# Attention stage: column sums through one shared PSUM bank, a split reciprocal, and a new DRAM order of the Q and K halves

## The chip, the cores and the metric

The kernel runs on one core of a Trainium2 chip. The metric is the device time of one execution in microseconds, as a median of runs. The engines named below are TensorE (PE, with its weight loads as PEld), VectorE (DVE), ScalarE (ACT), GpSimd (POOL) and SyncE (SP). SP does no arithmetic here; it issues all the DMAs. The core has 16 DMA engines.

## The reference

Two layers, each behind a group normalisation and with a residual. The first is a Mamba block (a scan over 4,096 positions, then an MLP), which the change does not touch. The second is self-attention over the same 4,096 positions, 8 heads of 32 channels, 2 images:

```python
x = x + _L0_conv_ref(_gn(x), ...)
x = x + _L1_conv_ref(_gn(x), L1_conv_qkv_w, L1_conv_qkv_b, 8)

# _L1_conv_ref; b = 2, c = 256, n = 64 * 64 = 4096, head_dim = 32
qkv = jnp.einsum('bchw,oc->bohw', x, qkv_w) + qkv_b[None, :, None, None]
qkv = qkv.reshape(b, 3, num_heads, head_dim, n)
q, k, v = (qkv[:, 0], qkv[:, 1], qkv[:, 2])
attn_logits = jnp.einsum('bhci,bhcj->bhij', q, k) * scale
attn_weights = jax.nn.softmax(attn_logits, axis=-1)
out = jnp.einsum('bhij,bhcj->bhci', attn_weights, v)
```

All of it is float32.

## The kernel before

The two images run one after the other. Each takes three stages: statistics and the Mamba block, then `prepare()` of the attention, then the main loop of the attention. The names below are those of `attention_block`.

**prepare().** It goes over NT = 8 tiles of T = 512 positions. A tile's normalised input `xn` (512 KB) comes from DRAM; PE makes Q and K (L552) and V (L578). For Q (`i = 0`) and K (`i = 1`), ACT rounds the result into a first half (L563) and DVE takes what is left over as a second half (L564), both in `halves`, a pool with two buffers. The two halves together carry the float32 value through the fast matmul type. Each half of each group of four heads, 128 channels by 512 positions or 256 KB, is stored to the DRAM tensor `scratch.qk` by one DMA (L573): 8 DMAs a tile, 64 an image. DRAM holds a half as 128 channels by 4,096 positions. V stays on the chip, and is stored to `scratch.v` by two DMAs of 2 MB after the last tile (L589); only a fallback path that these inputs never enter reads it.

**Stacks.** For the logits, a head's 32 channels are stacked four times on the 128 partitions: for keys as first, first, second, second half, for queries as first, second, first, second half. One matmul over 128 partitions then adds up all four products of halves. `load_stack` builds such a tile of 4 heads by 512 positions (1 MB) with four DMAs of 32 partitions each (L496), in rows of 512 floats (2 KB).

**Main loop.** A step is 128 keys against 512 queries for the four heads of a group. A query tile has NC = 32 steps, an image 16 tiles: group 0 is tiles 0 to 7, group 1 is tiles 8 to 15. In step c of a tile, ACT makes the exponentials of the step (two of 128x1024, L647), PE adds the step before to the output (`values`, L656, into `po`), pieces of `finish` run, PE makes the logits of the next step (L633, four matmuls into two PSUM tiles `s` of two banks, of which there are two buffers), and DVE and POOL add the exponentials up (`add_up`). The column sums are split: DVE adds the first two heads into `acc` in PSUM (L678); the third head goes to DVE in even steps (L680, third bank of `acc`) and to POOL in odd steps; the fourth goes to POOL.

**finish.** After a tile, `finish` runs in the first steps of the next one: DVE copies `acc` and `po` to SBUF (L694, L696), SP loads the residual `res` (L698), PE adds the sums over the partitions with five matmuls by ones into a tile `s` taken from the logits' ring (L704), DVE copies them out (L708), takes their maximum and their reciprocal (L711, L713), ACT adds a bias to `res` (L714), POOL multiplies and adds (L717, L718), SP stores the result (L719).

**Order.** `manual_schedule` keeps the order in which the main loop is written, engine by engine; each engine runs its own list in order. SP's list holds every DMA, and each DMA also waits for the one eight places before it, since eight completion semaphores go round. Keys of group 0 are loaded ahead of the loop; keys of group 1 are loaded in tile 7, one key tile every four steps, as the old ones come free (NT + 1 buffers); queries are loaded one tile ahead.

PSUM is full: `s` 2 x 2 banks, `acc` 3, `po` 1.

Of the kernel before, what the change touches and what calls it, by code (L numbers as in the profile page):

```python
# [475 lines left out]
class Scratch:  # L476
# [1 line left out]


    def __init__(self, pool, groups, L):  # L480
        self.qk = pool.tile([groups, 2, 2, P, L], F32, name="qk_dram")
        self.v = pool.tile([groups, P, L // P, P], F32, name="v_dram")
        self.x = pool.tile([groups, P, L], F32, name="x_dram")

# [5 lines left out]
def load_stack(nc, dst, src, which):  # L490

    for i in range(4):
        half = i // 2 if which else i % 2
        nc.sync.dma_start(  # L496
            dst[i * D : (i + 1) * D, :, :].bitcast(F32),
            src[half].rearrange("(h c) t -> c h t", c=D),
        )


@with_exitstack
def attention_block(ctx, tc, b, stats, consts, w, out, scratch, range_t):
# [14 lines left out]
    wp = ctx.enter_context(tc.tile_pool(name=f"l1w{b}", bufs=1))  # L518
    ps_s = ctx.enter_context(tc.tile_pool(name=f"l1pss{b}", bufs=2, space=PSUM))
    ps_a = ctx.enter_context(tc.tile_pool(name=f"l1psa{b}", bufs=1, space=PSUM))  # L520
    ps_o = ctx.enter_context(tc.tile_pool(name=f"l1pso{b}", bufs=1, space=PSUM))


# [10 lines left out]
    def prepare():  # L534

        with tc.tile_pool(name=f"l1p{b}", bufs=2) as p2:
# [3 lines left out]
            for t in range(NT):  # L540
                cols = bass.ts(t, T)
                xn = p2.tile([P, KC, T], F32, name="xn")
                nc.sync.dma_start(xn, x.rearrange("(k p) l -> p k l", p=P)[:, :, cols])
                for c in range(KC):
                    nc.vector.tensor_scalar(
                        xn[:, c, :], xn[:, c, :], gn[c][:, 0:1], gn[c][:, 1:2], ALU.subtract, ALU.mult
                    )
                for i in range(2):
                    pm = s_tile()
                    for m in range(KC):  # L550
                        for c in range(KC):
                            nc.tensor.matmul(  # L552
                                pm[:, m, :],
                                lhsT=w_qkv[:, c, bass.ds(i * C + m * P, P)],
                                rhs=xn[:, c, :],
                                start=(c == 0),
                                stop=(c == KC - 1),
                            )

                    halves = p2.tile([P, 2, KC, T], F32R, name="halves")  # L560
                    for m in range(KC):
                        bias = b_qkv[:, i * KC + m : i * KC + m + 1]
                        nc.scalar.activation(halves[:, 0, m, :], pm[:, m, :], AF.Identity, bias=bias)  # L563
                        nc.vector.scalar_tensor_tensor(  # L564
                            halves[:, 1, m, :],
                            pm[:, m, :],
                            bias,
                            halves[:, 0, m, :].bitcast(F32),
                            ALU.add,
                            ALU.subtract,  # L570
                        )
                        for s in range(2):
                            nc.sync.dma_start(scratch.qk[b * KG + m, i, s, :, cols], halves[:, s, m, :].bitcast(F32))  # L573
                pm = s_tile()
                flat = pm.rearrange("p a t -> p (a t)")
                for j in range(T // P):
                    for c in range(KC):
                        nc.tensor.matmul(  # L578
                            flat[:, bass.ts(j, C)],
                            lhsT=xn[:, c, bass.ts(j, P)],  # L580
                            rhs=w_qkv[:, c, 2 * C : 3 * C],
                            start=(c == 0),
                            stop=(c == KC - 1),
                        )
                nc.vector.tensor_copy(
                    v[:, bass.ts(t, T // P), :].rearrange("p s c -> p (s c)"), flat
                )
            for g in range(KG):
                nc.sync.dma_start(scratch.v[b * KG + g], v[:, :, g * P : (g + 1) * P])  # L589

    prepare()

# [10 lines left out]
        pass  # L603

    S = KG * NT * NC
    todo = {}
    keys = {}
    queries = {}
# [2 lines left out]

    def load_keys(g, t):
        k = keys[g, t] = kp.tile([P, 4, T], F32R, name="k")
        load_stack(nc, k, scratch.qk[b * KG + g, 1, :, :, bass.ts(t, T)], 1)

    def load_queries(i):
        if i < KG * NT:
            g, t = divmod(i, NT)
            q = queries[i] = p2.tile([P, 4, T], F32R, name="q")
            load_stack(nc, q, scratch.qk[b * KG + g, 0, :, :, bass.ts(t, T)], 0)  # L620

    def logits(s):
        if s >= S:
# [41 lines left out]
    def add_up(s):  # L665
# [2 lines left out]
        tile_ = tiles[i]  # L668
        ea, eb = todo[s].e
        if c == 0:  # L670
            tile_.acc = ps_a.tile([P, 3, T], F32, name="acc")
            tile_.acc_p = p2.tile([P, 2, T], F32, name="acc_p")
            nc.vector.tensor_copy(tile_.acc[:, 0:2, :], ea)
            nc.vector.tensor_copy(tile_.acc[:, 2, :], eb[:, 0, :])
            nc.gpsimd.tensor_copy(tile_.acc_p[:, 1, :], eb[:, 1, :])
            return
        acc, acc_p = tile_.acc, tile_.acc_p
        nc.vector.tensor_add(acc[:, 0:2, :], acc[:, 0:2, :], ea)  # L678
        if c % 2 == 0:
            nc.vector.tensor_add(acc[:, 2, :], acc[:, 2, :], eb[:, 0, :])  # L680
            nc.gpsimd.tensor_add(acc_p[:, 1, :], acc_p[:, 1, :], eb[:, 1, :])  # L681
        elif c == 1:
            nc.gpsimd.tensor_copy(acc_p[:, 0, :], eb[:, 0, :])
            nc.gpsimd.tensor_add(acc_p[:, 1, :], acc_p[:, 1, :], eb[:, 1, :])
        else:
            nc.gpsimd.tensor_add(acc_p, acc_p, eb)  # L686
# [1 line left out]
    def finish(i):  # L688
# [2 lines left out]
        d = tiles[i]  # L691
        cols = bass.ts(t, T)
        acc = p1.tile([P, 3, T], F32, name="acc_sb")
        nc.vector.tensor_copy(acc, d.acc)  # L694
        po = p1.tile([P, T], F32, name="po_sb")
        nc.vector.tensor_copy(po, d.po)  # L696
        res = p2.tile([P, T], F32, name="res")
        nc.sync.dma_start(res, x[g * P : (g + 1) * P, cols])  # L698
        yield
        ps = s_tile()  # L700
        for h in range(4):
            parts = ((acc[:, 0, :],), (acc[:, 1, :],), (acc[:, 2, :], d.acc_p[:, 0, :]), (d.acc_p[:, 1, :],))[h]
            for n, part in enumerate(parts):
                nc.tensor.matmul(  # L704
                    ps[h * D : (h + 1) * D, 0, :], lhsT=ones, rhs=part, start=(n == 0), stop=(n == len(parts) - 1)
                )
        sums = p1.tile([P, T], F32, name="sums")
        nc.vector.tensor_copy(sums, ps[:, 0, :])  # L708
        yield
        at = b * KG * NT + i  # L710
        nc.vector.tensor_reduce(range_t[:, 0, at : at + 1], sums, AX.X, ALU.max)  # L711
        r = p1.tile([P, T], F32, name="r")
        nc.vector.reciprocal(r, sums)  # L713
        nc.scalar.activation(res, res, AF.Identity, bias=b_qkv[:, 2 * KC + g : 2 * KC + g + 1])  # L714
        yield
        nc.vector.tensor_reduce(range_t[:, 1, at : at + 1], r, AX.X, ALU.max)
        nc.gpsimd.tensor_mul(po, po, r)  # L717
        nc.gpsimd.tensor_add(res, res, po)  # L718
        nc.sync.dma_start(out[g * P : (g + 1) * P, cols], res)  # L719

    with tc.manual_schedule():
        load_keys(0, 0)
        load_queries(0)
        for t in range(1, NT):
            load_keys(0, t)
        logits(0)
# [1 line left out]
        while s <= S or side.waiting:  # L728
            i, c = divmod(s, NC)
            if s < S:  # L730
# [3 lines left out]
                if i % NT == NT - 1 and i < KG * NT - 1 and c % (T // P) == 0:  # L734

                    load_keys(i // NT + 1, c * P // T)
                exponentials(s)
            if 0 < s <= S:
                values(s - 1)
                if c == 0:  # L740
# [31 lines left out]
def attention_any_range(ctx, tc, consts, w, out, scratch):  # L772
# [1 line left out]

    nc = tc.nc
    ident = consts[0]
    groups, _, _, _, L = scratch.qk.shape
    B, C, _ = out.shape
    NT = L // T
    NC = L // P  # L780
# [10 lines left out]
    ones = p1.tile([P, D], F32, name="g_ones")  # L791
    nc.vector.memset(ones, 1.0)
    with tc.For_i(0, groups, 1) as g:
        k = p1.tile([P, 4, L], F32R, name="g_k")
        load_stack(nc, k, scratch.qk[bass.ds(g, 1), 1].rearrange("o s c t -> (o s) c t"), 1)
        v = p1.tile([P, NC, P], F32, name="g_v")
        nc.sync.dma_start(v, scratch.v[bass.ds(g, 1)].rearrange("o p s c -> (o p) s c"))
        bias = p1.tile([P, 1], F32, name="g_bias")
        nc.vector.tensor_copy(bias, bv.rearrange("p b g -> p (b g)")[:, bass.ds(g, 1)])
        with tc.For_i(0, L, T) as t:  # L800
            q = p1.tile([P, 4, T], F32R, name="g_q")
            load_stack(nc, q, scratch.qk[bass.ds(g, 1), 0, :, :, bass.ds(t, T)].rearrange("o s c t -> (o s) c t"), 0)
            o = p1.tile([P, T], F32, name="g_o")
            x = p1.tile([P, T], F32, name="g_x")
            nc.sync.dma_start(x, scratch.x[bass.ds(g, 1), :, bass.ds(t, T)].rearrange("o c t -> (o c) t"))
            for h in range(4):

                def logits(c):
                    s = ps.tile([P, T], F32, name="g_s")
                    nc.tensor.matmul(s, lhsT=k[:, h, bass.ts(c, P)], rhs=q[:, h, :], start=True, stop=True)  # L810
                    return s

                top = p1.tile([P, T], F32, name="g_top")
# [28 lines left out]
            nc.sync.dma_start(out[bass.ds(g, 1), :, bass.ds(t, T)].rearrange("o c t -> (o c) t"), o)  # L842


@with_exitstack
# [69 lines left out]
```

## Time and profile before

| | us |
|---|---|
| median of 3 runs (lowest, highest) | 5318.35 (5317.25, 5322.41) |
| the profiled execution, its own time | 5313.31 |
| its span, first to last instruction | 5311.5 |
| first image: statistics and Mamba | 0 to 1345 |
| first image: `prepare()` and the turn to the main loop | 1345 to 1472 |
| first image: main loop, 16 tiles | 1472 to 2655 |
| second image: the same stages | 2655, 3995, 4122, 5311 |

In the main loop of the first image (1183 us) PE is busy for 1168.7 us, ACT for 1005.8, POOL for 960.2, DVE for 924.6, and the DMA engines for 16% of their time. In the 127 us of `prepare()` the DMA engines are busy for 71% of their time, at 229 GB/s.

How to read it: the share of an engine over the whole span mixes three stages with different limits. What the change touches lies in `prepare()`, in the turn to the main loop, and in the first 15 steps of each tile.

### The profile page before, as it was taken

What the parts mean: (1) busy time and instruction counts of PE and PEld (TensorE: products, weight loads), DVE (VectorE), ACT (ScalarE), POOL (GpSimd) and SP (SyncE); (2) the same over time, 40 slices, a digit from 0 to 9 for tenths busy, and PEclk for the clock granted to TensorE, in tenths of its full rate; (3) what the DMA queues carried; (4) which work ended last, traced back from release to release, by engine and by line L of the source; (5) the groups of instructions that cost most, each with busy time, mean ns of one, the idle gap of its engine ahead of it and who ended that gap; (6) DMA issues with size and microseconds to landing.
All of it is one profiled execution on the core that took longest, in us unless ns stands there. A gap on an engine that the chain in (4) does not pass through costs nothing.

```text
span 5311.5 us, 55374 instructions
## 1 busy us (share of the span) xinstructions
PE 4696.1 (88%) x18018; PEld 1807.1 (34%) x18018; DVE 4320.2 (81%) x4210; ACT 3525.7 (66%) x4200; POOL 3522.9 (66%) x2494
## 2 busy tenths in 40 slices
PE   4788888888899999999947888888887999999998
PEld 1233333333433333333312333333334333333332
DVE  6999999997368777877769999999973777777887
ACT  4466665554278888888744666655541888888887
POOL 3665666665078888888736666666650788888887
PEclk8999999999999999999969999999998999999999
DMA  3122222211541113111031122222116411131110
GB/s 104 59 63 66 64 66 68 68 59 54 199 92 25 25 31 70 25 25 27 19 94 59 61 68 64 66 68 67 59 54 209 83 25 25 33 67 25 25 27 7
DMA packets 194106, 317.39 MB, mean 60 GB/s; under 512 B 28816, under 2 KB 48400, under 8 KB 193584
## 3 DMA queue, kind: packets, MB, share of 16 engines
q1 hardware_dynamic: 193808, 313.77, 20.8%
q8 instruction: 143, 2.34, 0.2%
q14 instruction: 155, 1.27, 0.1%
HBM read 254.46 MB, written 59.24 MB: 59 GB/s over the span
## 4 chain that ended last, share of the span: by engine, by line
PE 51%; POOL 17%; DVE 15%; issue 10%; ACT 3%; DMA 2%; SPq 1%; POOLq 0%; DVEq 0%; ACTq 0%
PE s L633 23%; PE po L656 19%; POOL h L418 12%; DVE h L413 8%; DVE dbu L409 3%; PE mm L186 2%; PE s L552 2%; PE y L429 2%; ACT da L402 1%; PE s L704 1%; POOL dt L322 1%; POOL sp_l L321 1%; PE s L578 1%; POOL state L417 1%; POOL dtu L323 1%
## 5 line engine op out<-in xcount | busy, mean ns | idle before, releaser
L647 ACT ACTIVATE e<-s 128x1024 f32<-128x1024 f32 x2048 | 1990.4, 1022 | 378.4 <-PE s L633 365.0
L678 DVE TENSOR_TENSOR acc<-acc,e 128x1024 f32<-128x1024 f32 x992 | 1221.6, 1231 | 419.0 <-ACT e L647 363.3
L633 PE MATMUL s<-q,k 128*128 128x512 f32 x4096 | 1328.6, 438 | 63.4 <-DMA q<-qk_dram 47.9
L413 DVE TENSOR_TENSOR_SCAN h<-da,state,dbu 128x512 f32<-128x512 f32 x1024 | 1255.0, 1267 | 51.4 <-DVE dbu L409 1.9
L686 POOL TENSOR_TENSOR acc_p<-acc_p,e 128x1024 f32<-128x1024 f32 x480 | 1147.2, 2390 | 222.2 <-ACT e L647 211.8
L418 POOL TENSOR_TENSOR h<-h,cn 128x1024 f32<-128x1024 f32 x512 | 1208.3, 2360 | 41.5 <-POOL state L417 0.7
L656 PE MATMUL po<-e,v 128*32 128x512 f32 x8192 | 1094.5, 606 | 0.0
L633 PEld LDWEIGHTS s<-q,k 128*128 128x128 f32 x4096 | 615.7, 189 | 1190.3 <-ACT e L647 1095.3
L429 PE MATMUL y<-h,ident 128*128 128x512 f32 x2048 | 1016.6, 620 | 0.2
L402 ACT ACTIVATE da<-dt,neg_a 128x512 f32<-128x512 f32 x1024 | 674.7, 713 | 295.9 <-DVE h L413 294.6
L681 POOL TENSOR_TENSOR acc_p<-acc_p,e 128x512 f32<-128x512 f32 x480 | 618.2, 1288 | 104.0 <-ACT e L647 68.9
L409 DVE TENSOR_TENSOR dbu<-dtu,bn 128x1024 f32<-128x1024 f32 x512 | 626.4, 1223 | 24.3 <-PE bn L394 5.3
L417 POOL COPY state<-h 128x2 f32<-128x2 f32 x512 | 96.6, 189 | 807.3 <-DVE h L413 774.4
L394 PE MATMUL bn<-projs,pick 112*128 112x512 f32 x512 | 304.5, 595 | 326.1 <-DVE dbu L409 325.2
L429 PEld LDWEIGHTS y<-h,ident 128*128 128x128 f32 x2048 | 405.2, 198 | 340.6 <-issue 309.8
L680 DVE TENSOR_TENSOR acc<-acc,e 128x512 f32<-128x512 f32 x480 | 336.0, 700 | 50.9 <-DVE acc L678 0.9
L394 PEld LDWEIGHTS bn<-projs,pick 112*128 112x128 f32 x512 | 99.0, 193 | 628.9 <-DVE dbu L409 541.3
L656 PEld LDWEIGHTS po<-e,v 128*32 128x32 f32 x8192 | 161.7, 108 | 375.3 <-issue 362.6
L186 PE MATMUL mm<-yn,w 128*128 128x512 f32 x512 | 248.0, 607 | 36.8 <-ACT hid L360 15.9
L186 PE MATMUL mm<-yn,w_in 128*128 128x512 f32 x512 | 251.2, 615 | 20.7 <-DVE u L300 13.4
L368 PE MATMUL mm<-hid,w 128*128 128x512 f32 x512 | 240.7, 597 | 14.4 <-DVE z L334 12.9
L360 ACT ACTIVATE hid<-mm,b 128x512 f32<-128x512 f32 x128 | 88.0, 687 | 196.8 <-PE mm L186 195.8
(125 smaller groups left out, 3469.0 us busy)
## 6 DMA issues: line engine op xcount, KB each, us to landing
cn<-c_dram SPq DMA_DIRECT2D x512, 256.0 KB, 3.1
qk_dram<-halves SPq DMA_DIRECT2D x128, 256.0 KB, 2.1
k<-qk_dram SPq DMA_DIRECT2D x128, 256.0 KB, 6.7
q<-qk_dram SPq DMA_DIRECT2D x128, 256.0 KB, 5.0
x_first<-in_x SPq DMA_DIRECT2D x16, 512.0 KB, 5.3
x_front<-in_x SPq DMA_DIRECT2D x16, 512.0 KB, 4.8
x_back<-in_x SPq DMA_DIRECT2D x16, 512.0 KB, 4.7
x_dram<-x_back SPq DMA_DIRECT2D x16, 512.0 KB, 3.0
```

Of the source, the lines that this page charges most:

```text
L186: nc.tensor.matmul(out, lhsT=lhsT, rhs=rhs, start=(i == 0), stop=(i == len(pairs) - 1))
L402: nc.scalar.activation(da[:, j, :], tiles[t].dt[q][:, j, :], AF.Exp, scale=neg_a[:, k, n : n + 1])
L409: nc.vector.tensor_tensor(dbu, tiles[t].dtu[q], s.bn.unsqueeze(1).to_broadcast([P, 2, T]), ALU.mult)
L413: nc.vector.tensor_tensor_scan(h[:, j, :], s.da[:, j, :], dbu[:, j, :], state[:, k, n : n + 1], ALU.mult, ALU.add)
L418: nc.gpsimd.tensor_tensor(h, h, s.cn.unsqueeze(1).to_broadcast([P, 2, T]), ALU.mult)
L429: nc.tensor.matmul(d.y[:, j, :], lhsT=ident, rhs=steps[g].h[:, j, :], start=False, stop=(n == N - 1))
L633: nc.tensor.matmul(ps[:, j, :], lhsT=keys[i // NT, kt][:, h, kj : kj + P], rhs=queries[i][:, h, :], start=True, stop=True,)
L647: nc.scalar.activation(e, d.s[half], AF.Exp, scale=SCALE)
L656: nc.tensor.matmul(tiles[i].po[h * D : (h + 1) * D, :], lhsT=v[:, c, g * P + h * D : g * P + (h + 1) * D], rhs=todo[s].e[h // 2][:, h % 2, :],
L678: nc.vector.tensor_add(acc[:, 0:2, :], acc[:, 0:2, :], ea)
L681: nc.gpsimd.tensor_add(acc_p[:, 1, :], acc_p[:, 1, :], eb[:, 1, :])
L686: nc.gpsimd.tensor_add(acc_p, acc_p, eb)
```

## The change

1. **Sums.** `acc` has two banks. The third bank becomes a pool `ps_2` of one bank under one tag: `acc_2` (the third head's sum) and `sums_ps` (the sums over the partitions, before in a tile `s`) take turns in it. So `acc_2` begins only at step 6: DVE takes the third head in the 13 even steps from 6 on, POOL in the others. POOL makes its first sum at step 1 from the exponentials of steps 0 and 1.
2. **finish.** DVE copies `acc` and `acc_2` in two instructions; ACT copies `po`. The reciprocal is made in four parts of 128 columns, one every second step; sums, maximum, parts, product and sum are spread over steps 0 to 15 instead of 0 to 3.
3. **DRAM order.** `scratch.qk` holds, for each group, Q or K, tile and half, a block of 32 channels by 4 heads by 512 positions, as a stack needs it. A half is stored by one DMA as before, now written 4 heads x 32 channels x 512 positions on the DRAM side. A stack is loaded by two DMAs of 64 partitions and rows of 2,048 floats (8 KB) instead of four: a query tile as 64 rows in one piece, a key tile as one block of 32 rows read twice (a leading dimension of 2 with step 0).
4. **Order on SP.** The queries of tile 0 are loaded before the keys. The two stores of V move from the end of `prepare()` to the first two steps of tile 1.
5. The fallback path's indices follow the new order; it is not entered.

```diff
-        self.qk = pool.tile([groups, 2, 2, P, L], F32, name="qk_dram")
+        self.qk = pool.tile([groups, 2, L // T, 2, D, 4, T], F32, name="qk_dram")
...
-    for i in range(4):
-        half = i // 2 if which else i % 2
-        nc.sync.dma_start(
-            dst[i * D : (i + 1) * D, :, :].bitcast(F32),
-            src[half].rearrange("(h c) t -> c h t", c=D),
-        )
+    src = src.rearrange("s c h t -> s c (h t)")
+    dst = dst.rearrange("p h t -> p (h t)").bitcast(F32)
+    for i in range(2):
+        rows = dst[2 * i * D : 2 * (i + 1) * D, :]
+        if which:
+            nc.sync.dma_start(rows, src[i].unsqueeze(0).to_broadcast([2, *src.shape[1:]]))
+        else:
+            nc.sync.dma_start(rows, src.rearrange("s c x -> (s c) x"))
...
+    ps_2 = ctx.enter_context(tc.tile_pool(name=f"l1ps2{b}", bufs=1, space=PSUM))
...
-                            nc.sync.dma_start(scratch.qk[b * KG + m, i, s, :, cols], halves[:, s, m, :].bitcast(F32))
+                            nc.sync.dma_start(
+                                scratch.qk[b * KG + m, i, t, s].rearrange("c h t -> h c t"),
+                                halves[:, s, m, :].bitcast(F32),
+                            )
...
-            for g in range(KG):
-                nc.sync.dma_start(scratch.v[b * KG + g], v[:, :, g * P : (g + 1) * P])
...
+    SHARED = range(6, NC, 2)
...
-            tile_.acc = ps_a.tile([P, 3, T], F32, name="acc")
+            tile_.acc = ps_a.tile([P, 2, T], F32, name="acc")
...
-            nc.vector.tensor_copy(tile_.acc[:, 2, :], eb[:, 0, :])
-            nc.gpsimd.tensor_copy(tile_.acc_p[:, 1, :], eb[:, 1, :])
+            nc.vector.tensor_copy(tile_.acc, ea)
+            tile_.eb0 = eb
...
+        if c == 1:
+            nc.gpsimd.tensor_add(acc_p, tile_.eb0, eb)
+        elif c in SHARED:
+            if c == SHARED[0]:
+                tile_.acc_2 = ps_2.tile([P, T], F32, name="acc_2", tag="a2")
+                nc.vector.tensor_copy(tile_.acc_2, eb[:, 0, :])
+            else:
+                nc.vector.tensor_add(tile_.acc_2, tile_.acc_2, eb[:, 0, :])
...
-        nc.vector.tensor_copy(acc, d.acc)
+        nc.vector.tensor_copy(acc[:, 0:2, :], d.acc)
+        nc.vector.tensor_copy(acc[:, 2, :], d.acc_2)
...
-        nc.vector.tensor_copy(po, d.po)
+        nc.scalar.copy(po, d.po)
...
-        ps = s_tile()
+        ps = ps_2.tile([P, T], F32, name="sums_ps", tag="a2")
...
+        yield
...
-        nc.vector.tensor_copy(sums, ps[:, 0, :])
+        nc.vector.tensor_copy(sums, ps)
+        nc.scalar.activation(res, res, AF.Identity, bias=b_qkv[:, 2 * KC + g : 2 * KC + g + 1])
...
+        yield 2
         r = p1.tile([P, T], F32, name="r")
-        nc.vector.reciprocal(r, sums)
-        nc.scalar.activation(res, res, AF.Identity, bias=b_qkv[:, 2 * KC + g : 2 * KC + g + 1])
-        yield
+        for j in range(T // P):
+            nc.vector.reciprocal(r[:, bass.ts(j, P)], sums[:, bass.ts(j, P)])
+            yield 2
...
-        load_keys(0, 0)
         load_queries(0)
+        load_keys(0, 0)
...
+            if i == 1 and c < KG:
+                nc.sync.dma_start(scratch.v[b * KG + c], v[:, :, c * P : (c + 1) * P])
```

More of the change, by code (lines that the diff above doesn't have):

```diff
@@ L613, in load_keys @@
         k = keys[g, t] = kp.tile([P, 4, T], F32R, name="k")
-        load_stack(nc, k, scratch.qk[b * KG + g, 1, :, :, bass.ts(t, T)], 1)
+        load_stack(nc, k, scratch.qk[b * KG + g, 1, t], 1)
     def load_queries(i):
@@ L619, in load_queries @@
             q = queries[i] = p2.tile([P, 4, T], F32R, name="q")
-            load_stack(nc, q, scratch.qk[b * KG + g, 0, :, :, bass.ts(t, T)], 0)
+            load_stack(nc, q, scratch.qk[b * KG + g, 0, t], 0)
     def logits(s):
@@ L670, in add_up @@
         if c == 0:
-            tile_.acc = ps_a.tile([P, 3, T], F32, name="acc")
+            tile_.acc = ps_a.tile([P, 2, T], F32, name="acc")
             tile_.acc_p = p2.tile([P, 2, T], F32, name="acc_p")
-            nc.vector.tensor_copy(tile_.acc[:, 0:2, :], ea)
-            nc.vector.tensor_copy(tile_.acc[:, 2, :], eb[:, 0, :])
-            nc.gpsimd.tensor_copy(tile_.acc_p[:, 1, :], eb[:, 1, :])
+            nc.vector.tensor_copy(tile_.acc, ea)
+            tile_.eb0 = eb
             return
         acc, acc_p = tile_.acc, tile_.acc_p
[L678 to L683, printed above, removed]
+        nc.vector.tensor_add(acc, acc, ea)
+        if c == 1:
[6 more added lines that the diff above has]
+                nc.vector.tensor_add(tile_.acc_2, tile_.acc_2, eb[:, 0, :])
             nc.gpsimd.tensor_add(acc_p[:, 1, :], acc_p[:, 1, :], eb[:, 1, :])
@@ L704, in finish @@
                 nc.tensor.matmul(
-                    ps[h * D : (h + 1) * D, 0, :], lhsT=ones, rhs=part, start=(n == 0), stop=(n == len(parts) - 1)
+                    ps[h * D : (h + 1) * D, :], lhsT=ones, rhs=part, start=(n == 0), stop=(n == len(parts) - 1)
                 )
+        yield
         sums = p1.tile([P, T], F32, name="sums")
-        nc.vector.tensor_copy(sums, ps[:, 0, :])
+        nc.vector.tensor_copy(sums, ps)
+        nc.scalar.activation(res, res, AF.Identity, bias=b_qkv[:, 2 * KC + g : 2 * KC + g + 1])
         yield
@@ L711, in finish @@
         nc.vector.tensor_reduce(range_t[:, 0, at : at + 1], sums, AX.X, ALU.max)
+        yield 2
         r = p1.tile([P, T], F32, name="r")
-        nc.vector.reciprocal(r, sums)
-        nc.scalar.activation(res, res, AF.Identity, bias=b_qkv[:, 2 * KC + g : 2 * KC + g + 1])
-        yield
+        for j in range(T // P):
+            nc.vector.reciprocal(r[:, bass.ts(j, P)], sums[:, bass.ts(j, P)])
+            yield 2
         nc.vector.tensor_reduce(range_t[:, 1, at : at + 1], r, AX.X, ALU.max)
         nc.gpsimd.tensor_mul(po, po, r)
+        yield 2
         nc.gpsimd.tensor_add(res, res, po)
@@ L721, in attention_block @@
     with tc.manual_schedule():
+        load_queries(0)
         load_keys(0, 0)
-        load_queries(0)
         for t in range(1, NT):
@@ L776, in attention_any_range @@
     ident = consts[0]
-    groups, _, _, _, L = scratch.qk.shape
+    groups, _, L = scratch.x.shape
     B, C, _ = out.shape
@@ L793, in attention_any_range @@
     with tc.For_i(0, groups, 1) as g:
-        k = p1.tile([P, 4, L], F32R, name="g_k")
-        load_stack(nc, k, scratch.qk[bass.ds(g, 1), 1].rearrange("o s c t -> (o s) c t"), 1)
+        k = p1.tile([P, NT, 4, T], F32R, name="g_k")
+        for t in range(NT):
+            load_stack(nc, k[:, t], scratch.qk[bass.ds(g, 1), 1, t].rearrange("o s c h t -> (o s) c h t"), 1)
         v = p1.tile([P, NC, P], F32, name="g_v")
@@ L799, in attention_any_range @@
         nc.vector.tensor_copy(bias, bv.rearrange("p b g -> p (b g)")[:, bass.ds(g, 1)])
-        with tc.For_i(0, L, T) as t:
+        with tc.For_i(0, NT, 1) as t:
             q = p1.tile([P, 4, T], F32R, name="g_q")
-            load_stack(nc, q, scratch.qk[bass.ds(g, 1), 0, :, :, bass.ds(t, T)].rearrange("o s c t -> (o s) c t"), 0)
+            load_stack(nc, q, scratch.qk[bass.ds(g, 1), 0, bass.ds(t, 1)].rearrange("o n s c h t -> (o n s) c h t"), 0)
             o = p1.tile([P, T], F32, name="g_o")
             x = p1.tile([P, T], F32, name="g_x")
-            nc.sync.dma_start(x, scratch.x[bass.ds(g, 1), :, bass.ds(t, T)].rearrange("o c t -> (o c) t"))
+            nc.sync.dma_start(x, scratch.x[bass.ds(g, 1), :, bass.ds(t * T, T)].rearrange("o c t -> (o c) t"))
             for h in range(4):
@@ L809, in logits @@
                     s = ps.tile([P, T], F32, name="g_s")
-                    nc.tensor.matmul(s, lhsT=k[:, h, bass.ts(c, P)], rhs=q[:, h, :], start=True, stop=True)
+                    nc.tensor.matmul(s, lhsT=k[:, c * P // T, h, c * P % T : c * P % T + P], rhs=q[:, h, :], start=True, stop=True)
                     return s
@@ L841, in attention_any_range @@
             nc.vector.scalar_tensor_tensor(o, o, bias, x, ALU.add, ALU.add)
-            nc.sync.dma_start(out[bass.ds(g, 1), :, bass.ds(t, T)].rearrange("o c t -> (o c) t"), o)
+            nc.sync.dma_start(out[bass.ds(g, 1), :, bass.ds(t * T, T)].rearrange("o c t -> (o c) t"), o)
 @with_exitstack
```

## The prediction

> **What bounds the kernel now.** I read the page first, then busy times by stretch, then the order of time around the turn to the main loop and a tile's end, then the DMA issues. Stretches first (columns: length, busy time and instructions of PE, PEld, DVE, ACT, POOL, granted clock, DMA share, GB/s):
>
> ```profile
> 1345.00:1472.00 127.00, 92.07 (x272) 52.52 (x271) 44.54 (x68) 24.98 (x36) 0.12 (x1) 0.86 0.71 229
> 1472.00:2655.00 1183.00, 1168.71 (x6304) 396.51 (x6302) 924.58 (x865) 1005.82 (x1041) 960.22 (x559) 0.99 0.16 35
> 1366.00:1372.00 6.00, 6.00 (x23) 4.18 (x22) 2.85 (x4) 2.06 (x3) 0.00 (x0) 1.00 0.77 286
> 1472.00:1500.00 28.00, 27.74 (x138) 9.80 (x137) 18.69 (x18) 23.28 (x24) 18.46 (x12) 0.91 1.06 210
> ```
>
> The main loop is PE's: 1168.7 of 1183 us, with transfers at 16%. `prepare()` is different: PE sets its pace, but inside it the DMA engines are already 77% busy (third line). Transfers that take longer there, or load keys more slowly than the loop eats them, become the bound.
>
> The turn to the main loop, in order of time (start, length):
>
> ```profile
> 1429.38 18.05 SPq L573 DMA_DIRECT2D qk_dram<-halves  x16
> ...
> 1448.76 6.05 SPq L589 DMA_DIRECT2D v_dram<-v  x2
> 1455.05 9.64 SPq L496 DMA_DIRECT2D q<-qk_dram  x4
> ...
> 1471.50 2.05 PE L633 MATMUL s<-q,k 128*128 128x512 f32 x4 [24.04 <-DMA q<-qk_dram]
> ```
>
> The V stores stand ahead of the first queries; PE idles 24.04 us. The trace puts 47.9 us on this wait over both images. At a tile's end:
>
> ```profile
> 1544.58 1.76 DVE L694 COPY acc_sb<-acc 128x1536 f32<-128x1536 f32 x1
> ...
> 1546.66 1.94 ACT L647 ACTIVATE e<-s 128x1024 f32<-128x1024 f32 x2 [0.18 <-PE s L633]
> ...
> 1550.67 1.96 ACT L647 ACTIVATE e<-s 128x1024 f32<-128x1024 f32 x2 [2.07 <-PE s L633]
> ...
> 1550.77 0.30 PEld L633 LDWEIGHTS s<-q,k 128*128 128x128 f32 x2 [0.57 <-DVE sums L708]
> ...
> 1552.52 0.71 ACT L714 ACTIVATE res<-res,b_qkv 128x512 f32<-128x512 f32 x1
> ```
>
> A usual step takes 2.2 us, here 4.01 (1546.66 to 1550.67): PE spends about 2 us on the sums, and 0.57 us waiting for DVE to free the borrowed `s`. From the copy at 1544.58 to the last tile's at 2645.41 are 15 tiles, 73.4 us each. ACT needs `res` 8 us after a tile's end; once, in the second image, it came late and ACT stood:
>
> ```profile
> 4643.26 0.72 ACT L714 ACTIVATE res<-res,b_qkv 128x512 f32<-128x512 f32 x1 [3.89 <-DMA res<-x_dram]
> ```
>
> **The change, part by part.** All sums are for the first image, then doubled.
>
> *Sums and finish.* The five matmuls stay on PE. What goes is the 0.57 us wait: 17.2 us over the run by the trace. ACT's waits for DVE and POOL to free exponentials (6.3 and 5.3 us in the run) can shrink too. POOL gets 18 sums of 2.39 us and 13 of 1.29 a tile, 59.8 us, for 57.7 before; it has some 220 us of slack an image. DVE loses two sums of 0.70 us; four reciprocals cost 3.34 us plus three starts of perhaps 0.16 (its 128x1 reciprocal). Both engines run beside PE. `po` on ACT (0.68 us as on DVE) starts exponentials of step 1 at 1547.16, not 1546.66; PE is at the sums until 1549.97, which hides it. Uncovered it would cost 0.68 x 32 = 22 us in the run, against a gain of at most 17.2 + 11.6 = 29. I take -9 us an image.
>
> *Stores of the halves.* As many DMAs and 2 KB rows as before, but the DRAM side's outermost dimension is now 4, where it was 128. Every DMA of the trace has an outermost count of 16, 112 or a multiple of 32, so it shows no such store. Two rows (columns: count, size, us to landing):
>
> ```profile
> c_dram<-cc SPq DMA_DIRECT2D x16, 32.0 KB, 1.6
> qk_dram<-halves SPq DMA_DIRECT2D x128, 256.0 KB, 2.1
> ```
>
> The first stores 16 rows of 2 KB, the second 128. If 16 rows were one to an engine and 128 eight, the difference is seven rows in 0.5 us: 71 ns a row, 1.5 us fixed. The stretch at 1366 says 286 / (16 x 0.77) = 23.2 GB/s an engine, 88 ns a row. They agree, so a split by the outermost index fits; I take 80 ns. For four outermost indices the cost lies between two ends: spread over 16 engines as every row here, no change; or one index to an engine, 32 rows x 80 ns = 2.56 us on the same four. The nearest row is the first, where the outermost count sets how many engines work, so I take the far end. Then 64 stores take 163.8 us, and the six `xn` loads behind the first stores 16 rows each, 7.7 us. From the first store (1365.84 + 1.5) the last lands at 1538.8; before, at 1447.43 + 2.1 = 1449.5. PE needs 10.6 us a tile and hides nothing of 21.8.
>
> The Trainium skill, page "DMA: Bandwidth & Descriptors", section "Why a DMA increments its semaphore by 16 and not by 1", speaks against this change: the queue takes the largest number up to 16 that divides both sides' outermost counts, the lowest-numbered engines first. By it the stores run on 4 engines, the key loads on 2, the query loads on 16, and the sum is the forecast's; by the rows' other end it is the first rival's. No run here has yet shown a DMA below 16.
>
> *Loads.* In the changed program's order the first queries wait for all eight completion counters, so for the last store: 1538.8. Two DMAs of 64 rows of 8 KB over 16 engines: eight rows each, at 0.32 us (four times 80 ns) 2.6 us. A key DMA has 64 rows, but its DRAM side begins with a dimension of 2 (step 0): 32 rows on each of two engines, 10.24 us, 20.5 for a tile's two. Ends: over 16 engines, 2.6 us a tile; or at the rate an engine had while 16 read keys (210 / (16 x 1.06) = 12.4 GB/s), 42 us. That rate seems a limit of the sum, 210 GB/s, and two engines ask for 51; I take 20.5. First logits at 1538.8 + 1.5 + 2.6 + 20.5 = 1563.4 (1471.5 before). Four steps eat a key tile in 8.9 us, so tile 0 waits for each: the eighth lands 7 x 20.5 = 143.4 later, tile 0 ends at 1715.7 instead of 1544.6: **+171**.
>
> *V stores.* Off the turn, but in tile 1 `res` stands behind one: 1.5 + 2.6 (queries) + 2 MB / 287 GB/s = 7.3 + 0.6 = 12 us after the tile's start, needed at 8: **+4**. The stores themselves have no reader.
>
> *Keys of group 1.* In tile 7, `res` is issued after the first key tile and on two engines lies behind it: 1.5 + 2.6 + 20.5 + 0.6 = 25, needed at 8: **+17**; ACT stands, and behind it PE. The next key tile is asked for at 10.8 + 17 = 28 us, the others 8.9 apart, faster than 20.5: the last lands at 28 + 1.5 + 143.4 = 173 after tile 7's start. Tile 8 starts at 73.4 + 17 = 90.4; its `res`, behind all keys, lands at 174, needed at 98.4: **+76**.
>
> *Sum.* 171 + 4 + 17 + 76 - 9 = +259 us an image, +518. Span 5311.5 + 518 = 5829.5; with the 1.8 outside it in its own time (5313.31) 5831; the median lies 5.0 above that run: **5836**. With 71 ns it is 5724, with 88 ns 5936.
>
> **The rivals.**
> *All transfers spread over 16 engines* (not slower). For it: every DMA of the trace. Against: none has fewer than 16 outermost indices. Queries start at 1449.5; 2 MB take 5.1 us (25.6 GB/s x 16) to 10 (210 GB/s), so the first logits come 10 to 15 us earlier, 13 taken. -13 + 4 - 9 = -18 an image: 5282, faster; a gain of nothing in finish and a later `res` would make it no change.
> *A tile's two key DMAs take different engines.* Then 10.2 us a tile, and tile 0 ends at 1633.7 (+89), tiles 7 and 8 lose 7 and 3: +94 an image, 5506. Against: nothing seen alternates.
> *Only the key loads are narrow*, the store's queue splitting its second dimension: first logits at 1474.1, tile 0 +82, the rest as forecast, +170 an image: 5658.
> *Keys at 12.4 GB/s an engine*: +608 an image, about 6534; the row exists, but with sixteen readers.
>
> **How the numbers follow.** Forecast 0.74, all spread 0.10, different engines 0.06, only keys 0.04, slow keys 0.06. The likeliest's own range is 5724 to 5936; rates a little worse than 88 ns, and the 5506 case, stretch it to 5490 to 6060, which leaves out the first and last rivals and a rest. A difference of 0.2%, about 11 us, is what a measurement can tell from none. Only the first rival is not slower: 0.08 faster, 0.02 the same; 0.90 slower.
>
> **What would show it.** The key loads' time to landing (6.7 us now) should exceed 10, the stores' (2.1) too as they queue; the stretch of `prepare()` should run at a DMA share near a quarter with PE waiting; the first logits should come near 1563; PE should wait for keys in tile 0, and ACT for `res` in tiles 7 and 8. Landings near 3 us and first logits before 1465 would mean the spread is kept, and the forecast falls. The wait for DVE's sums copy (17.2 us) should be gone either way.

## The result, and the profile after

The changed kernel takes 5904.81 us (median of 4 runs, 5900.71 to 5906.95); the kernel before took 5319.15 beside it (4 runs, 5317.25 to 5322.41). The ratio is 1.1099, 95% interval 1.108 to 1.1119: 11% slower. The profiled execution has a span of 5898.9 us, 587.4 more than before's, or 293.7 an image.

Lines of the profile's page of after (busy us of each engine, its share of the span in brackets, then the count of its instructions):

```profile
span 5898.9 us, 54608 instructions
PE 4768.4 (81%) x18018; PEld 1846.3 (31%) x18018; DVE 4193.5 (71%) x4210; ACT 3531.2 (60%) x4232; POOL 3582.9 (61%) x2430
DMA packets 165045, 317.32 MB, mean 54 GB/s; under 512 B 24337, under 2 KB 43921, under 8 KB 156337
```

The same lines of before:

```profile
PE 4696.1 (88%) x18018; PEld 1807.1 (34%) x18018; DVE 4320.2 (81%) x4210; ACT 3525.7 (66%) x4200; POOL 3522.9 (66%) x2494
DMA packets 194106, 317.39 MB, mean 60 GB/s; under 512 B 28816, under 2 KB 48400, under 8 KB 193584
```

The bytes are those of before, in fewer packets, at 54 GB/s instead of 60. No engine's busy time grew by anything near 587 us (PE's by 72, POOL's by 60). So the time must be in waits, and the table of waits says whose (columns: engine, tile, line, what it waited for; total us over both images, times, longest):

```profile
...
PE s L638 <- DMA k<-qk_dram: 240.2, 15, 57.8
...
ACT res L718 <- DMA res<-x_dram: 198.2, 7, 72.8
DVE xn L548 <- DMA xn<-x_dram: 184.2, 16, 18.6
...
ACT halves L566 <- DMA qk_dram<-halves: 129.9, 15, 9.4
```

All four are waits for transfers: key loads, residuals queued behind key loads, and in `prepare()` inputs and buffers held up by stores. The rows overlap in time, so they aren't added up. The wait of PE's weight loads for DVE's copy of `sums` at the end of a tile (17.2 us before) is gone from this table.

Where the 293.7 us of the first image went can be read from one instruction of `finish`, ACT's bias on `res`, which runs once a tile:

| mark | before | after | difference |
|---|---|---|---|
| first mark (tile 1, step 3 or so) | 1552.5 | 1761.0 | +208.5 |
| interval that holds tile 7's late `res` | 75.8 | 93.3 | +17.5 |
| next interval (tile 8) | 74.5 | 146.5 | +72.0 |
| an undisturbed interval | 72.8 | 72.6 | -0.2 |

These make 298.0; the other tiles and the last interval (66.1 for 68.2) give back the rest. The 75.8 of before holds a late `res` too, by 2.92 us. Of the first difference 1.1 us is the mark itself, which the new `finish` places later (1553.65 in e5 below).

`prepare()` and the turn to the main loop of after, by stretches (columns as in the prediction: length, PE, PEld, DVE, ACT, POOL, clock, DMA share, GB/s):

```profile
1345.00:1595.00 250.00, 107.65 (x280) 62.28 (x279) 44.19 (x69) 24.41 (x36) 0.12 (x1) 0.71 0.29 98
1410.00:1435.00 25.00, 12.08 (x32) 7.08 (x32) 5.04 (x7) 2.64 (x4) 0.00 (x0) 0.80 0.31 110
1600.00:1700.00 100.00, 54.51 (x241) 20.15 (x239) 28.96 (x28) 38.66 (x40) 38.03 (x20) 0.76 0.13 53
```

The stage that took 127 us takes 250. In one of its tiles (second line) PE is busy for 12 of 25 us and the DMA engines for 31%. In tile 0 of the main loop (third line) they are busy for 13%: 0.13 x 16 = 2.1 engines, at 53 / 2.1 = 25 GB/s each, and PE works half the time. Everything waits for DMA engines of which most stand idle.

SP's list in the same stretch (start, length of a block of issues):

```profile
1384.21 22.15 SPq L576 DMA_DIRECT2D qk_dram<-halves  x8
1406.46 2.36 SPq L546 DMA_DIRECT2D xn<-x_dram  x1
1408.91 22.34 SPq L576 DMA_DIRECT2D qk_dram<-halves  x8
...
1507.49 42.16 SPq L576 DMA_DIRECT2D qk_dram<-halves  x16
1560.55 1.20 SPq L501 DMA_DIRECT2D q<-qk_dram  x2
```

From 1384.21 to 1507.49 are five tiles, 24.7 us each, where PE's work is 10.6. Then the logits, in order of time (start, length, and in brackets the idle time before with its cause):

```profile
1593.80 2.04 PE L638 MATMUL s<-q,k 128*128 128x512 f32 x4 [57.37 <-DMA k<-qk_dram]
...
1613.49 2.04 PE L638 MATMUL s<-q,k 128*128 128x512 f32 x4 [9.67 <-DMA k<-qk_dram]
```

A key tile comes every 20 us (the next was at 1633.98); before the change, PE had its first logits at 1471.50 and kept going. ACT's waits for `res`, in tiles 1, 7 and 8:

```profile
1761.01 0.72 ACT L718 ACTIVATE res<-res,b_qkv 128x512 f32<-128x512 f32 x1 [4.91 <-DMA res<-x_dram]
...
2218.34 0.72 ACT L718 ACTIVATE res<-res,b_qkv 128x512 f32<-128x512 f32 x1 [20.61 <-DMA res<-x_dram]
...
2364.89 0.72 ACT L718 ACTIVATE res<-res,b_qkv 128x512 f32<-128x512 f32 x1 [72.82 <-DMA res<-x_dram]
```

The profile's page also counts engines without any timing. Read that a DMA ends with one packet of 4 bytes from each engine that took part: before's 1,097 DMAs at 16 make 17,552, and 17,552 completions are what its trace holds. If after's 128 stores use 4 engines, its 64 key loads 2 and its other 777 DMAs 16, there are 512 + 128 + 12,432 = 13,072, which is 4,480 fewer. The packets under 512 B went from 28,816 to 24,337: 4,479 fewer. Packets of exactly 4 bytes on the DMA queue, counted in the two traces, went from 25,744 to 21,264: 4,480 fewer.

### The profile page after: what moved, and what is told of

It is laid out like the page before. It is cut to its first block, busy times and chain, and to the rows that moved or that the text cites. A ratio compares the mean times of both kernels' runs of the same rounds, so it can differ in the third digit from the quotient of the medians.

```text
span 5898.9 us, 54608 instructions
## 1 busy us (share of the span) xinstructions
PE 4768.4 (81%) x18018; PEld 1846.3 (31%) x18018; DVE 4193.5 (71%) x4210; ACT 3531.2 (60%) x4232; POOL 3582.9 (61%) x2430
## 2 busy tenths in 40 slices
DMA packets 165045, 317.32 MB, mean 54 GB/s; under 512 B 24337, under 2 KB 43921, under 8 KB 156337
## 4 chain that ended last, share of the span: by engine, by line
PE 41%; POOL 16%; DVE 13%; issue 10%; DMA 8%; SPq 7%; ACT 4%; POOLq 0%; DVEq 0%; ACTq 0%
PE s L638 19%; PE po L661 15%; POOL h L418 12%; DVE h L413 6%; SPq L499 5%; DVE dbu L409 3%; DMA xn<-x_dram 3%; DMA res<-x_dram 3%; PE mm L186 2%; DMA k<-qk_dram 2%; PE y L429 1%; ACT da L402 1%; POOL dt L322 1%; ACT e L652 1%; POOL sp_l L321 1%
## 5 line engine op out<-in xcount | busy, mean ns | idle before, releaser
L638 PE MATMUL s<-q,k 128*128 128x512 f32 x4096 | 1343.3, 443 | 448.2 <-DMA k<-qk_dram 240.2
L693 POOL TENSOR_TENSOR acc_p<-acc_p,e 128x1024 f32<-128x1024 f32 x544 | 1298.7, 2387 | 493.7 <-ACT e L652 481.8
L638 PEld LDWEIGHTS s<-q,k 128*128 128x128 f32 x4096 | 633.4, 192 | 1578.7 <-ACT e L652 1280.0
L661 PE MATMUL po<-e,v 128*32 128x512 f32 x8192 | 1107.8, 613 | 0.0
L691 POOL TENSOR_TENSOR acc_p<-acc_p,e 128x512 f32<-128x512 f32 x416 | 533.8, 1283 | 151.1 <-ACT e L652 119.6
L684 POOL TENSOR_TENSOR acc_p<-e 128x1024 f32<-128x1024 f32 x32 | 75.9, 2370 | 554.8 <-ACT e L652 308.4
L186 PE MATMUL mm<-yn,w_in 128*128 128x512 f32 x512 | 251.1, 615 | 20.6 <-DVE u L300 13.3
L690 DVE TENSOR_TENSOR acc<-acc,e 128x512 f32<-128x512 f32 x384 | 264.8, 690 | 0.0
```

The lines of the kernel that those rows point to most:

```text
L186: nc.tensor.matmul(out, lhsT=lhsT, rhs=rhs, start=(i == 0), stop=(i == len(pairs) - 1))
L638: nc.tensor.matmul(ps[:, j, :], lhsT=keys[i // NT, kt][:, h, kj : kj + P], rhs=queries[i][:, h, :], start=True, stop=True,)
L661: nc.tensor.matmul(tiles[i].po[h * D : (h + 1) * D, :], lhsT=v[:, c, g * P + h * D : g * P + (h + 1) * D], rhs=todo[s].e[h // 2][:, h % 2, :],
```

## The experiments

The theory: a DMA uses as many engines as the outermost counts of its two sides allow, so a store with 4 outermost uses four, a key load that begins with a dimension of 2 uses two; both cost their full bytes over those engines, and nothing else of the change matters at this scale. The rivals: the DRAM layout itself is slow (rows of 8 KB, or scattered 2 KB rows); the new order on SP is what hurts; the new `finish` hurts. The first four runs stood beside a kernel before of 5315.56 us (11 runs, 5311.12 to 5318.67), the last three beside 5315.16 (21 runs, 5311.31 to 5321.39); after's own 5904.81 stood beside 5319.15, so a difference to it carries some 4 us of that.

### Key loads wide, stores as they are (e1_wide_keys)

```diff
-            nc.sync.dma_start(rows, src[i].unsqueeze(0).to_broadcast([2, *src.shape[1:]]))
+            for r in range(2):
+                nc.sync.dma_start(rows[r * D : (r + 1) * D, :], src[i])
```

Same bytes, same 8 KB rows, same DRAM layout; only the leading 2 is gone, at the price of twice as many DMAs.

> The changed kernel with each key DMA (64 partitions, leading dimension 2 with step 0) cut into two of 32 rows of 8 KB, so the outermost count is 32 on both sides; stores stay narrow. Theory (as many engines as the outermost counts allow): a key tile takes some 3 to 10 us instead of 20.5, so tile 0 lasts about 72 us instead of 155, the first logits come about 20 us earlier, and ACT no longer waits 20 and 73 us for res in tiles 7 and 8: about 198 us less an image, 5505 us (5480 to 5530). Rival (the cost lies in the longer rows or the new blocks, not in the number of engines): no change, 5900.

Measured 5517.61 us (one run): 387 us of the 586 are gone. The waits of PE for keys fall to two, the first logits of each image, and `prepare()` is untouched:

```profile
PE s L639 <- DMA k<-qk_dram: 73.6, 2, 36.9
```

The packets under 512 B rise by 1,919; 128 key loads at 16 for 64 at 2 is 1,920. While keys stream in beside the loop, the stretch of this kernel reads:

```profile
1576.00:1600.00 24.00, 24.00 (x131) 7.89 (x129) 14.68 (x14) 20.83 (x22) 20.58 (x10) 0.98 1.02 223
```

PE is busy all the time, sixteen engines work, at 223 GB/s. So 8 KB rows of this layout are not slow in themselves.

### Stores wide, key loads as they are (e2_wide_stores)

The columns of the Q and K weights (and their biases) are permuted on the chip to (channel, head) order, so that the partitions of `halves` already stand in DRAM order. The store then writes the same DRAM rows with 128 outermost.

```diff
+            w_qk = p2.tile([P, KC, 2 * C], F32, name="w_qk", bufs=1)
+            for c in range(KC):
+                nc.gpsimd.tensor_copy(
+                    w_qk[:, c, :].rearrange("p (g d h) -> p g h d", d=D, h=4),
+                    w_qkv[:, c, 0 : 2 * C].rearrange("p (g h d) -> p g h d", d=D, h=4),
+                )
...
-                                lhsT=w_qkv[:, c, bass.ds(i * C + m * P, P)],
+                                lhsT=w_qk[:, c, bass.ds(i * C + m * P, P)],
...
-                                scratch.qk[b * KG + m, i, t, s].rearrange("c h t -> h c t"),
+                                scratch.qk[b * KG + m, i, t, s].rearrange("c h t -> (c h) t"),
```

> The changed kernel with the Q and K columns of the weights put in stack order on the chip (one POOL copy per image and weight block), so a half leaves SBUF in the order of its DRAM block and its store has 128 rows on both sides; same DRAM layout, keys stay narrow. Theory: the stores spread over 16 engines, prepare() runs at 10.6 us a tile instead of 24.5, the first queries are issued near 1450 instead of 1560: about 108 us less an image, 5690 us (5665 to 5715). Rival (the stores are slow because of where the rows land): no change, 5900.

Measured 5691.72 us (one run): 213 us gone, and `prepare()` is PE's again. Its stretch, and the two waits that remain:

```profile
1360.00:1445.00 85.00, 80.81 (x236) 45.27 (x237) 37.74 (x52) 19.91 (x29) 1.91 (x2) 0.96 0.62 218
```

```profile
ACT res L728 <- DMA res<-x_dram: 201.0, 6, 72.6
...
PE s L648 <- DMA k<-qk_dram: 184.7, 14, 35.3
```

PE is busy for 81 of 85 us. `res` still waits behind the keys on two engines, for as long as in after.

### Both wide (e3_wide_both)

The two edits together, to see whether anything of the loss is left.

> Both mends together: the changed kernel's sums, finish, DRAM blocks, 8 KB rows and order, with no DMA below 16 outermost indices. Theory: below the kernel before by what is gained at the turn (10 to 15 us an image) and in finish (0.8 us a tile), less a late res in tile 1: 5285 us (5270 to 5305). Rival (longer rows or blocks cost something of their own): above 5318.

Measured 5301.89 us (8 runs, 5298.61 to 5305.47), ratio 0.9976, interval 0.9965 to 0.9987: the whole loss is gone and a little more. The two edits alone bring back 387 + 213 = 600 us, together 603, so the two losses hardly overlap. The turn came as forecast: first logits at 1460.31, 11.2 us earlier than in before. The forecast of 5285 was still too low: `finish` is worth 4.9 us an image (e5, below) where it counted 0.8 a tile, and V's stores still delay `res` in tile 1. In tile 7 the keys of group 1 delay it by 4.20 us, not much more than in before (2.92). One line shows V's part:

```profile
1545.68 0.72 ACT L729 ACTIVATE res<-res,b_qkv 128x512 f32<-128x512 f32 x1 [4.99 <-DMA res<-x_dram]
```

### Stores with two heads (e4_two_heads)

A dose: if the outermost count sets the engines, halving it doubles the time of the stores, though bytes, rows and addresses stay.

```diff
-                            nc.sync.dma_start(
-                                scratch.qk[b * KG + m, i, t, s].rearrange("c h t -> h c t"),
-                                halves[:, s, m, :].bitcast(F32),
-                            )
+                            for h in range(0, 4, 2):
+                                nc.sync.dma_start(
+                                    scratch.qk[b * KG + m, i, t, s].rearrange("c h t -> h c t")[h : h + 2],
+                                    halves[h * D : (h + 2) * D, s, m, :].bitcast(F32),
+                                )
```

> The changed kernel with each store cut into two of two heads: 64 partitions, outermost count 2 on the DRAM side. Twice the DMAs, the same rows. Theory, with the same lowest engines each time: two engines carry 64 rows a store pair each, 43 us a tile instead of 21.5, about 172 us more an image: 6245 us (6200 to 6300). Rival (each DMA takes other engines): two DMAs of two engines fill four, no change, 5900; rival (the number of DMAs costs): about 0.5 us of SP a store, some 4 us a tile, 5970.

Measured 6259.71 us (one run), another 355 on top. SP's list in `prepare()`; a block of 32 is two tiles:

```profile
1461.21 74.92 SPq L577 DMA_DIRECT2D qk_dram<-halves  x32
1536.23 2.87 SPq L546 DMA_DIRECT2D xn<-x_dram  x2
1556.50 73.22 SPq L577 DMA_DIRECT2D qk_dram<-halves  x32
```

Two tiles take 95.3 us, 47.6 each, for 24.7 in after: nearly twice. The packets under 512 B are 24,337, the same number as in after: 256 stores at 2 make 512, as 128 at 4 did. Scattered rows would have cost the same as in after; a price per DMA alone was expected at about 5970; and if each DMA took other engines, two stores would have filled four and the time would have stayed.

### The new finish alone (e5_finish_only)

The kernel before with parts 1 and 2 of the change (the third bank shared, `po` on ACT, the reciprocal in four parts) and with its old DRAM layout and order:

```diff
-            tile_.acc = ps_a.tile([P, 3, T], F32, name="acc")
+            tile_.acc = ps_a.tile([P, 2, T], F32, name="acc")
...
-        ps = s_tile()
+        ps = ps_2.tile([P, T], F32, name="sums_ps", tag="a2")
...
-        nc.vector.reciprocal(r, sums)
+        for j in range(T // P):
+            nc.vector.reciprocal(r[:, bass.ts(j, P)], sums[:, bass.ts(j, P)])
+            yield 2
```

> The kernel before with parts 1 and 2 of the change alone (sums in the shared bank, finish spread over 15 steps, po on ACT, reciprocal in four parts); DRAM order, loads and SP's order as before. Theory: the 0.57 us wait for the sums copy goes, but PE keeps its five sum matmuls, so a tile falls from 72.8 to 72.6 us and the tail after the last tile by 1 to 2 us: 4 to 6 us an image, about 10 us in all, 5306 us (5300 to 5312) beside 5316. Rival (finish was the gain of the change): 9 us an image or more, below 5299.

Measured 5305.32 us (11 runs, 5302.44 to 5311.08), ratio 0.9983, interval 0.9974 to 0.9992: 9.8 us gained. A tile takes 72.6 us instead of 72.8, the last interval of an image 66.1 instead of 67 to 68. The wait of 0.57 us a tile is gone, but only 0.2 of it is gained. The copy of `po` on ACT is no new wait for PE: its loads for the next `values` waited for the copy on DVE just as long (first line before, second e5):

```profile
PEld po L656 <- DVE po_sb L696: 10.9, 30, 0.4
```

```profile
PEld po L658 <- ACT po_sb L701: 10.9, 30, 0.4
```

Where the other 0.4 us a tile go, no run separates.

### The new order alone (e6_order_only)

The kernel before with the queries loaded ahead of the keys and V's stores in tile 1, nothing else:

```diff
-            for g in range(KG):
-                nc.sync.dma_start(scratch.v[b * KG + g], v[:, :, g * P : (g + 1) * P])
...
-        load_keys(0, 0)
         load_queries(0)
+        load_keys(0, 0)
...
+            if i == 1 and c < KG:
+                nc.sync.dma_start(scratch.v[b * KG + c], v[:, :, c * P : (c + 1) * P])
```

> The kernel before with part 4 alone: the first queries ahead of the keys, the V stores in tile 1. Theory: the first queries no longer stand behind 4 MB of V stores, but the first key tile, loaded during prepare() before, now comes after them, so first logits near 1461 instead of 1471.5; ACT waits 3 to 5 us for res in tile 1: 5 to 8 us less an image, 5303 us (5297 to 5310). Rival (the V stores hurt as much in tile 1 as at the turn): 5316, no change.

Measured 5309.93 us (11 runs, 5304.94 to 5314.44), ratio 0.9987, interval 0.9978 to 0.9996: 5.2 us gained, less than the 12 expected and close to the edge of what can be told. The first logits come 7.1 us earlier (1464.39; near 1461 was expected), and tile 1 loses most of that again:

```profile
1464.39 2.04 PE L631 MATMUL s<-q,k 128*128 128x512 f32 x4 [14.39 <-DMA k<-qk_dram]
```

```profile
1550.22 0.72 ACT L712 ACTIVATE res<-res,b_qkv 128x512 f32<-128x512 f32 x1 [5.14 <-DMA res<-x_dram]
```

PE's idle time at the turn is 14.39 us instead of 24.04; then `res` is 5.14 us late behind V's stores. With e5's 9.8 us this makes 15.0, and e3, which has both and the new DRAM order besides, gained 13.7: the blocks and rows of 8 KB brought nothing of their own that these runs can tell.

### All wide, and the residual early (e7_all_wide)

From e3: keys stacked as first, second, first, second half (two plain loads of 64 rows) and queries as first, second, second, first (three), which gives the same four products; keys ahead of queries; `res` loaded in step 24 of its own tile; V's stores in steps 16 and 17 of tile 1.

```diff
+    both = src.rearrange("s c x -> (s c) x")
+    nc.sync.dma_start(dst[0 : 2 * D, :], both)
+    if which:
+        nc.sync.dma_start(dst[2 * D : 4 * D, :], both)
+    else:
+        nc.sync.dma_start(dst[2 * D : 3 * D, :], src[1])
+        nc.sync.dma_start(dst[3 * D : 4 * D, :], src[0])
...
+            if s < S and c == 24:
+                tiles[i].res = p2.tile([P, T], F32, name="res")
+                g, t = divmod(i, NT)
+                nc.sync.dma_start(tiles[i].res, x[g * P : (g + 1) * P, bass.ts(t, T)])
+            if i == 1 and 16 <= c < 16 + KG:
+                g = c - 16
+                nc.sync.dma_start(scratch.v[b * KG + g], v[:, :, g * P : (g + 1) * P])
```

> The version with both mends, and with stacks in another order: keys first, second, first, second half in two plain DMAs of 64 rows, queries first, second, second, first in three, all on 16 engines; keys ahead of queries; res loaded in step 24 of its own tile; V stores in steps 16 and 17 of tile 1. Theory: first logits near 1455 (a key tile waits on chip, 1 MB of queries to load), no wait for res in tiles 1, 7 and 8: 10 to 14 us less an image than with the mends alone (5302), 5278 us (5268 to 5292). Rival (the extra waits in tiles 7 and 8 and at the start come from the 215 GB/s of the key loads themselves): above 5292.

Measured 5270.06 us (5 runs, 5269.15 to 5271.93), ratio 0.9914, interval 0.9901 to 0.9928: faster than both kernels, and than e3 by 31.8 us, all its parts together; none was run alone. No wait of ACT for `res` is left in its table, and every tile takes 72.6 us, 1, 7 and 8 among them. At the turn PE waits for the queries, now the later of the two, for 10.12 us (14.58 for keys in e3); the first logits come at 1462.53, where 1455 was expected:

```profile
1462.53 2.05 PE L649 MATMUL s<-q,k 128*128 128x512 f32 x4 [10.12 <-DMA q<-qk_dram]
```

## Why the prediction was right, and where its sizes were off

*The mechanism.* Four engines for a store and two for a key load were a choice between two ends. The two landing times gave the price of a row, 71 to 88 ns, but fit an even spread over 16 engines just as well, and no run then had a DMA below 16, so what decided was an argument. Now both counts stand on four things: the count of 4-byte packets, the 13% of tile 0, the time that came back when the outermost count was widened without touching a byte (e1 to e3), and the near doubling of the stores' time when it was halved (e4). That is for counts of 4 and 2; no other count below 16 was run. On the Trainium skill's page "DMA: Bandwidth & Descriptors", section "Why a DMA increments its semaphore by 16 and not by 1", only the engines that a DMA uses post a completion (for DMAs issued as here, from SP: HWDGE); the 4,479 fewer packets agree with that and with its rule for their number.

*Stores: mis-sized.* The forecast was 21.8 us a tile; it is 24.7. The rate was right. The DMA view of one tile of after, in 40 slices of 0.625 us:

```profile
GB/s 295 360 200 105 105 102 102 98 105 102 98 102 102 102 102 102 62 36 16 13 46 56 95 98 105 111 85 98 98 105 105 102 102 98 105 105 102 102 108 256
```

While the four engines write, 102 GB/s is 25.5 each, 80 ns for a row of 2 KB, the number that was used. The hole in the middle is what was left out: six slices at 13 to 62 instead of 102 miss 383 GB/s x 0.625 us, or 2.3 us of work. The two `halves` buffers are full, so ACT waits for stores to land; then `xn`, queued behind stores itself, comes late, and until PE, ACT and DVE have made the next half, the four engines have nothing to write. DVE's line at that place:

```profile
1418.66 0.55 DVE L548 TENSOR_SCALAR xn<-xn,gn_sc 128x512 f32<-128x512 f32 x1 [14.79 <-DMA xn<-x_dram]
```

The sum let eight tiles of stores follow each other without a gap. With the hole, the queries were issued at 1560.55 instead of 1538.8; some 2.4 us of it is a later first store (1368.21 for 1365.84).

*Turn: mis-sized.* From the first query's issue to the first logits the forecast had 24.6 us; it is 33.25. Together with the stores, the first logits came at 1593.8 for 1563.4, 30.4 us late, and this is nearly all that the forecast lacks: 293.7 - 259 = 34.7 an image. Doubled and added to 5836, the 30.4 give 5897, for 5904.81 measured. The section on the hardware shows where most of the 8.7 us lie.

*Key tiles: right.* 20.5 us were expected, 19.7 and 20.5 are seen; tile 0 lost 203.6 us (208.5 less the 4.9 of `res`), where the forecast's 171, the 30.4 us of late start and the 1.1 of the mark make 202.5.

*Waits for `res`: right.* Expected 4, 17 and 76 us in tiles 1, 7 and 8; ACT stood 4.9, 20.6 and 72.8. In tile 7 the forecast's own base was misread: `res` was late there in before as well, in both images (2.92 and 3.89 us) and not once, so 17.7 of the 20.6 are new. The reading is that a residual load uses all 16 engines and so can't land before the two that carry the keys have reached it; e1 fits, where the keys are wide and ACT's waits for `res` fall from 198.2 us to 18.4.

*Finish: too large.* Expected -9 us an image; alone it brings 9.8 in the run, 4.9 an image (e5). The waits went as said: the 17.2 us of PE's loads are gone, and ACT's 11.6 us for DVE and POOL fall to 1.6. But the run became only 9.8 us shorter; the forecast took waits for time, and what filled the rest stays open. (DVE loses three sums a tile, not two: 480 adds and 32 copies become 384 and 32. It runs beside PE, so nothing hangs on it.)

*The rivals.* All spread over 16: refuted by the packet count; made by hand in e3 it is 5301.89 and not 5282, for the smaller gain of finish and the late `res`. Different engines for the two key DMAs: refuted by 20 us a tile, where it needed 10.2. Only keys narrow: built as e2, 5691.72 for the 5658 worked out, again mostly for the slow turn (first logits at 1485.60, not 1474.1). Keys at 12.4 GB/s an engine: refuted by 53 GB/s on two.

*The signs.* Waits, late logits and late `res` came as listed; the DMA share in `prepare()` was 0.29 to 0.31, a little over a quarter. The times to landing, named first, can't be read: the DMA view of after lists none.

## What to carry to other kernels

Before rewriting a DMA for longer rows or fewer instructions, look at the outermost count of both its sides: here a leading 4 on a store and a leading 2 on a load cost 11% although bytes and issue count were no worse, and putting the long dimension first (by permuting weight columns, or by two plain loads for one that repeats) took it all back. Count who queues behind a narrow transfer too: loads that used all engines were late by up to 72.8 us because two of their sixteen were taken. And a residual that is needed right after a tile's end should be asked for inside the tile: together with V's stores moved off the tile's start and plain stacks it brought 31.8 us here.

## What the hardware showed that was not expected

The first key tile after the queries came slowly, though its loads have the form of the later ones, which got a mean of 53 GB/s on two engines. The DMA view of after from 1560 to 1600, in slices of 1 us:

```profile
GB/s 0 57 188 279 221 205 131 33 16 33 33 33 33 33 25 41 25 49 25 49 33 33 49 41 49 57 49 49 57 49 57 49 49 57 57 49 49 57 49 57
```

The queries take the first seven slices at up to 279 GB/s. Then the loads get 33 GB/s for some ten slices, 16 for each of two engines instead of 26, and settle only near 1585: up to there they are some 6 us short of 53 GB/s, most of the 8.7 us that the forecast lacks at the turn. PE, ACT and DVE are idle then, and SP's list shows only key loads. In the second image, in e2 and in e4 it is the same. When the keys of group 1 follow a burst in tile 7, it is so again in the second image, but in the first only some three slices are slow. The cause stays open: no run here separated it.

Longer rows brought no bandwidth: sixteen engines read key stacks at 210 GB/s with rows of 2 KB (before) and at 223 with rows of 8 KB (e1), 13 to 14 GB/s an engine, while two engines alone get 26 each. What limits the sum at that place was not tried.
